# Moving loads of x, weights and first residuals in a cross-attention kernel

## The chip, the cores and the metric

The kernel runs on one core of a Trainium2 chip. The metric is device time in microseconds: the median of three runs. Beside it there is one profiled execution, whose time and span are given with it. The core's engines are PE (matrix products), DVE (reductions, transposes), ACT (ScalarE: copies out of PSUM, exponentials), POOL (elementwise work) and SP, which here only issues DMAs. ACT can issue DMAs too, in the order of its own instructions.

## What is computed

Two batches of 2048 tokens with 640 channels attend over 154 context rows, in 20 heads of 32 channels. The first 77 context rows and the last 77 have their own key and value weights and their own softmax; the two results are added, projected by Wo, and bias and residual are added.

```
q      = split_heads(x @ Wq.T)
k, v       = split_heads(text @ Wk.T),   split_heads(text @ Wv.T)     # context rows 0..76
k_ip, v_ip = split_heads(ip @ Wk_ip.T),  split_heads(ip @ Wv_ip.T)    # context rows 77..153
out = merge_heads(softmax(q k^T * s) v) + merge_heads(softmax(q k_ip^T * s) v_ip)
return out @ Wo.T + bo + x
```

## The kernel before

All matrices lie transposed in memory, channels first, in float32. Tokens are cut into four blocks of 1024 (`NBLK`), each of two halves of 512 (`TB`, `NH`). Channels are cut into five groups of 128 (`NC`), each of which is four heads (`G`).

The main loop has 20 iterations and one more to drain: iteration m handles block j = m // 5 and channel group c = m % 5. On PE it does the scores of 8 token tiles in three groups (3, 3 and 2 tiles, `scores(m, 0..2)`), and `attend(m - 1)`, the product of the iteration before's probabilities with V. Between those stands other PE work, which `plan(m)` lists in two parts, `after1` and `after2`. In iterations 0 to 4 these are a query projection for a later iteration, the V projections of group m, the K projections of group m + 1 and another query projection. Later they are query projections and output projections (`fill`). The order on every engine is the order of the program text; nothing reorders it.

ACT copies scores out of PSUM (`take`), computes the exponentials (`exponential`, part of `soften`), and copies queries, K, V and attention results out of PSUM. DVE does row maxima, sums, reciprocals, transposes of probabilities, and the last step of the output (`store`, line 319: PSUM result plus bias plus residual). POOL subtracts the maxima and multiplies by the reciprocals. A PSUM bank is used again once the engine that reads it is done; `turn_to` gives out the low or high four banks.

`soften(m, 0)` stands between the pieces of `after1`: the variable `ahead` says how many of them come first. Where `after1` has more than one entry, 2 < m < 18 and c > 0, the last entry comes behind `soften(m, 0)`. At c = 0 (iterations 5, 10, 15), where `after1` is two query projections, both come first.

Loads before the change:

- Weights of K and V: 20 tiles of 512 KB, through five slots that lie in the space of `aTs[1]`. `project_kv` issues the next load (`load_w`) right behind its matmuls.
- V, squared up by a DVE transpose (`square_v`), is spread over partitions by 16 small DMAs from SBUF to SBUF (`spread_v`, 20 KB each, called "pieces" below) for each channel group, and again for the second batch later.
- x of the next block: two loads of 1280 KB (`load_x(j + 1, h)`), written in iterations with c = 1, that is 1, 6 and 11.
- Wo: one load at the end of iteration 4. It goes into `wo_ct`, which held the context, so it waits for the last K and V projection.
- Residuals (`fetch`): 256 KB for each output tile; `flush` fetches up to `FETCH` = 3 ahead of the outputs stored so far, behind each store. There are 40 output tiles.

All of these are on SP's queue, in the order of the text; an issue that has to wait for a semaphore holds up every issue behind it. On ACT's queue there are only the first five loads of `wq`. The program gives all DMAs eight completion semaphores in turn, so each one also waits until the one eight places before it in program order has landed.

Of the kernel before, what the change touches and what calls it, by code (L numbers as in the profile page):

```python
# [19 lines left out]
def kernel(  # L20
# [25 lines left out]
    nc = tc.nc  # L46
    P = 128
    NC = C // P
    NCC = CC // P
    G = P // D  # L50
    TB = 512
    NH = 2
    BLK = NH * TB
    NT = BLK // P
    NBLK = B * S // BLK
# [6 lines left out]
    NM = NBLK * NC  # L62
# [4 lines left out]
    FETCH = 3  # L67
# [12 lines left out]
    def turn_to(half, n=G):  # L80


        turn[:] = half[:1] if n == 1 else (half[: min(n, G) - 1] + half[-1:]) * 2

    def bank():
        return turn.pop(0)
# [5 lines left out]
    xs = [const.tile([P, NC, BLK], F32, name=f"x_{n}") for n in range(2)]  # L92
# [14 lines left out]
    wo = wo_ct.rearrange("p (k o) -> p k o", k=NC)  # L107
# [6 lines left out]
    def block_of(m):  # L114

        j, c = divmod(m, NC)
        return j, c, j * BLK // S
# [7 lines left out]
    def load_w():  # L125
        n = len(loaded)
        if n < len(wlist):
            src, c = wlist[n]
            w = wslots[n % len(wslots)]
            nc.sync.dma_start(  # L130
                out=w, in_=src[:, ts(c, P)].rearrange("(k p) o -> p k o", p=P)
            )
            loaded.append(w)

    def project_kv(n, t):

        out = bank()[:, : B * L].rearrange("p (b l) -> p b l", b=B)
        for k in range(NCC):
            nc.tensor.matmul(  # L139
                out, loaded[n][:, k, :], cT[:, k, :, t, :], start=(k == 0), stop=(k == NCC - 1)  # L140
            )
        load_w()
        return out

    def project_k(c, t):
        nc.scalar.copy(kT[:, c, :, t, :], project_kv(4 * c + t, t))  # L146

    def project_v(c, t):
        nc.scalar.copy(vTs[c % 2][:, :, ds(t * L, L)], project_kv(4 * c + 2 + t, t))

    def square_v(c):
        nc.vector.transpose(
            vS[:, c].rearrange("p b l -> p (b l)"),
            vTs[c % 2].rearrange("p b l -> p (b l)"),
        )

    def spread_v(c, b):

        for g in range(G):
            for r in range(G):  # L160
                nc.sync.dma_start(
                    out=v4[r * D : (r + 1) * D, c, g].rearrange("p k d -> p (k d)"),
                    in_=vS[g * D : (g + 1) * D, c, b],
                )


    def load_x(j, h):
        nc.sync.dma_start(
            out=xs[j % 2][:, :, ts(h, TB)],
            in_=xT[:, ds(j * BLK + h * TB, TB)].rearrange("(c p) s -> p c s", p=P),  # L170
        )

    qTs = {}

# [22 lines left out]
    def keys_of(m, s):  # L197
        return pb_of(m, s)[:, :, :, : 2 * L]
# [4 lines left out]
    def scores(m, s, ps):  # L203

        _, c, b = block_of(m)
        first, n = GROUPS[s]
        for t in range(n):
            h, st = divmod(first + t, TB // P)
            for g in range(G):
                nc.tensor.matmul(  # L210
                    ps[g][:, ts(t, 2 * L)],
                    qTs[(m, h)][g * D : (g + 1) * D, ts(st, P)],
                    kT[g * D : (g + 1) * D, c, b].rearrange("p t l -> p (t l)"),
                    start=True,
                    stop=True,
                )

    def take(m, s, ps):

        n = GROUPS[s][1]  # L220
        for g in range(G):
            nc.scalar.copy(  # L222
                keys_of(m, s)[:, :, g], ps[g][:, : n * 2 * L].rearrange("p (n l) -> p n l", n=n)
            )

    def maxima(m, s):
        n = GROUPS[s][1] * G
        mx = small.tile([P, n, 2], F32, tag=f"mx{n}", name=f"mx_{m}_{s}")
        nc.vector.tensor_reduce(mx, rows_of(m, s), AX.X, ALU.max)  # L229
        nc.gpsimd.tensor_tensor(  # L230
            rows_of(m, s), rows_of(m, s), mx.unsqueeze(3).to_broadcast([P, n, 2, L]), ALU.subtract
        )
# [21 lines left out]
    def soften(m, s):  # L254
        exponential(m, s)
        sums(m, s)
        normalise(m, s)

    def transpose(m, s):
        first, n = GROUPS[s]  # L260
        nc.vector.transpose(  # L261
            tT[:, first : first + n].rearrange("p n g k s -> p (n g k s)"),
            pb_of(m, s).rearrange("p n g l -> p (n g l)"),
        )
# [59 lines left out]
    outs = [Out(v) for v in range(NV)]  # L324
# [23 lines left out]
    def flush():  # L348
        for o in finished[len(stored) :]:
            o.store()  # L350
            stored.append(o)
            for o in outs[len(stored) : len(stored) + FETCH]:
                o.fetch()
# [15 lines left out]
    for k in (0, half):  # L369
        nc.sync.dma_start(  # L370
            out=wo_ct[:, ds(k * B * LT, half * B * LT)].rearrange("p (k n) -> p k n", k=half),
            in_=ctxT[ds(k * P, half * P), :].rearrange("(k p) n -> p k n", p=P),
# [17 lines left out]
    for t in range(2):  # L390
        project_k(0, t)

    def plan(m):

        q = [lambda h=h: queries(m + LEAD[h], h) for h in range(NH)]
        out = lambda: fill(NC)
        if m < NC:
            v = [lambda t=t: project_v(m, t) for t in range(2)]
            k = [lambda t=t: project_k(m + 1, t) for t in range(2) if m + 1 < NC]
            return q[:1] + v, k + q[1:]  # L400
        if m == NM - 1:
            return [out], [out] + [lambda: fill(NC - 1)] * OPEN
        if m == NM - 2:
            return [out], [out, q[1]]
        if m % NC == 0:
            return q, [out] * 2
        return [out, q[0]], [out, q[1]]

    def is_late(m):


        return m == NC or (m > NC and m % NC == 1)

    for m in range(NM + 1):
        j, c, _ = block_of(m)
        new = m < NM
        old = m >= 1
        after1, after2 = plan(m) if new else ([], [])
        flush()
        if new:  # L420
            for g, half in ((0, LOW), (1, HIGH)):
                scores(m, g, half)
            for g, half in ((0, LOW), (1, HIGH)):
                take(m, g, half)
        turn_to(LOW, len(after1))


        ahead = len(after1)
        if ahead > 1 and 2 < m < NM - 2 and c > 0:
            ahead -= 1  # L430
        short = new and (len(after1) == 1 or m == 0)
        late = is_late(m)
        if old and not late:
            transpose(m - 1, 2)
        if new:
            maxima(m, 0)
        if late:
            transpose(m - 1, 1)
        if new and not short:
            maxima(m, 1)  # L440
        if late:
            transpose(m - 1, 2)
        if c == 1 and j + 1 < NBLK:
            for h in range(NH):
                load_x(j + 1, h)
        for work in after1[:ahead]:
            work()
        flush()
        if new:
            if short:  # L450
                maxima(m, 1)
            else:
                soften(m, 0)
        for work in after1[ahead:]:
            work()
        flush()
        if m < NC:
            square_v(m)
            spread_v(m, 0)
        if new:  # L460
            scores(m, 2, HIGH)
        if old:
            attend(m - 1, LOW)
        if new:
            take(m, 2, HIGH)
            maxima(m, 2)
            if short:
                soften(m, 0)
                if old:
                    take_attention(m - 1, LOW)  # L470
            soften(m, 1)
            if short:
                soften(m, 2)
        if old:
            if not short:
                take_attention(m - 1, LOW)
            attended[(m - 1) // NC] += 1
            if (m - 1) // NC == NBLK // B - 1:
                spread_v((m - 1) % NC, 1)
        turn_to(HIGH, len(after2))  # L480
        if new:
            transpose(m, 0)
        for work in after2[:-1]:
            work()
        flush()
        if new and not short:
            soften(m, 2)
        for work in after2[-1:]:
            work()
        if m >= NC and (c == 0 or m == NM - 2):  # L490
            flush()
        if new and not is_late(m + 1):
            transpose(m, 1)
        if m == NC - 1:
            nc.sync.dma_start(out=wo, in_=WoT.rearrange("(c p) o -> p c o", p=P))
    turn_to(LOW)
    while len(finished) < NV:
        fill(NC)
# [33 lines left out]
```

## Time and profile before

| | us |
|---|---|
| median of 3 runs (lowest, highest) | 537.57 (536.95, 538.74) |
| the profiled execution | 538.22 |
| its span | 536.4 |
| PE works on the first projections from | 10.97 |
| first scores of iteration 0 | 24.6 |
| first scores of iteration 5 | 140.6 |
| last output matmuls end near | 532.8 |

The page gives busy time, shares and counts for each engine; a table of stretches gives the same for parts of the span, with the clock that PE was granted (1.00 is full) and the share of the 16 DMA engines that was busy. A matmul in float32 appears as two matmuls and two weight loads. A row of the timeline is: start, length, engine, line, operation, what it writes and reads, count, and in brackets the idle time of the engine before it and what ended that. "issue" there means that the profile shows nothing that the engine waited for. SPq and ACTq are the DMA issues of those engines. Some matmul records can be missing, so counts can be a few short.

DMA issues of the page that the change touches, with KB each and median us from issue to landing:

| load | issued by | count | KB | us |
|---|---|---|---|---|
| residuals | SP | 40 | 256 | 3.3 |
| x of the next block | SP | 6 | 1280 | 8.7 |
| V pieces | SP | 160 | 20 | 1.8 |
| weights of K, K_ip, V, V_ip | SP | 5 each | 512 | 7.0, 4.4, 5.5, 4.2 |
| Wo | SP | 1 | 1600 | 7.0 |

### The profile page before, as it was taken

The numbers are of one execution on the slowest core, as the hardware profiler recorded it, in microseconds if no ns is written. First come the engines' busy times: TensorE is split into PE (matmuls) and PEld (weight loads), VectorE is DVE, ScalarE is ACT, GpSimd is POOL, SyncE is SP. The second block draws the span as 40 slices with busy tenths as digits, with TensorE's granted clock in tenths as the row PEclk, the third lists the DMA queues.
The fourth block names the chain that finished last, engine by engine and source line by source line (L and its number), as shares of the span: only waits on it lengthen the run. The fifth ranks groups of instructions, "written<-read, shape, count | busy, mean of one in ns | idle before, by whom it ended". The sixth has DMA issues, their size and how long they took to land.

```text
span 536.4 us, 12754 instructions
## 1 busy us (share of the span) xinstructions
PE 522.8 (97%) x5614; PEld 289.0 (54%) x5614; DVE 378.1 (70%) x286; ACT 245.1 (46%) x441; POOL 351.0 (65%) x130
## 2 busy tenths in 40 slices
PE   8999799999999999999999999999999999999997
PEld 4676668677554545545454554544455454554442
DVE  0059765877878879787768978787678878888121
ACT  1255445456654444644454464445356464562000
POOL 0057947796967868668677866869576876978000
PEclk9999799999999999999999999999999999999999
DMA  8974733320136420221206311111112111131151
GB/s 258 308 208 138 243 94 88 97 59 9 32 138 221 150 89 25 82 65 48 57 16 221 144 41 40 42 39 42 38 41 75 45 42 40 40 101 40 61 187 67
DMA packets 50488, 50.60 MB, mean 94 GB/s; under 512 B 5248, under 2 KB 34432, under 8 KB 50432
## 3 DMA queue, kind: packets, MB, share of 16 engines
q1 hardware_dynamic: 49712, 49.45, 30.3%
q8 instruction: 44, 0.72, 0.6%
q10 hardware_dynamic: 720, 0.33, 0.2%
q14 instruction: 12, 0.10, 0.1%
HBM read 36.00 MB, written 10.49 MB: 87 GB/s over the span
## 4 chain that ended last, share of the span: by engine, by line
PE 87%; DVE 4%; issue 2%; DMA 2%; POOL 2%; ACT 1%; SPq 0%; ACTq 0%; DVEq 0%; POOLq 0%
PE bank L181 30%; PE bank L308 30%; PE bank L273 11%; PE bank L210 8%; PE bank L139 8%; DVE den L243 2%; POOL pb L250 2%; DVE mx L229 1%; DMA x<-in_x_dram 1%; ACT pb L236 1%; DVE ot L319 1%; DMA wq<-in_L_xattn_Wq_dram 1%; DMA res<-in_x_dram 1%; POOL pb L230 0%; DVE tT L261 0%
## 5 line engine op out<-in xcount | busy, mean ns | idle before, releaser
L230 POOL TENSOR_TENSOR pb<-pb,mx 128x1848 f32<-128x1848 f32 (+1 forms) x60 | 175.8, 2942 | 105.9 <-DVE mx L229 105.9
L250 POOL TENSOR_TENSOR pb<-pb,rden 128x1848 f32<-128x1848 f32 (+1 forms) x60 | 176.0, 2942 | 36.9 <-DVE rden L245 27.7
L181 PE MATMUL bank<-x,wq 128*128 128x512 f32 x400 | 180.0, 599 | 0.9 <-DMA x<-in_x_dram 0.9
L308 PE MATMUL bank<-aT,wo_ct 128*128 128x512 f32 x400 | 179.1, 599 | 0.9 <-ACT aT L285 0.9
L243 DVE TENSOR_REDUCE den<-pb 128x24 f32<-128x1848 f32 (+1 forms) x60 | 111.3, 1856 | 62.3 <-ACT pb L236 62.2
L229 DVE TENSOR_REDUCE mx<-pb 128x24 f32<-128x1848 f32 (+1 forms) x60 | 109.6, 1848 | 43.3 <-ACT pb L222 42.3
L236 ACT ACTIVATE pb<-pb 128x1848 f32<-128x1848 f32 (+1 forms) x60 | 95.1, 1587 | 87.4 <-POOL pb L230 87.4
L181 PEld LDWEIGHTS bank<-x,wq 128*128 128x128 f32 x400 | 75.4, 191 | 92.8 <-issue 87.4
L308 PEld LDWEIGHTS bank<-aT,wo_ct 128*128 128x128 f32 x400 | 73.7, 190 | 91.8 <-issue 83.8
L261 DVE STREAM_TRANSPOSE tT<-pb 128x1920 f32<-128x1920 f32 (+1 forms) x60 | 115.9, 1931 | 5.3 <-POOL pb L250 5.2
L222 ACT COPY pb<-bank 128x462 f32<-128x462 f32 (+1 forms) x240 | 101.1, 533 | 22.5 <-PE bank L210 21.2
L273 PE MATMUL bank<-tT,v 32*32 32x256 f32 x3200 | 70.5, 386 | 4.1 <-issue 3.6
L189 ACT COPY qT<-bank 128x512 f32<-128x512 f32 x40 | 23.4, 585 | 99.5 <-PE bank L181 99.5
L210 PEld LDWEIGHTS bank<-kT,qT 32*128 32x128 f32 x1280 | 44.7, 184 | 30.2 <-issue 19.6
L273 PEld LDWEIGHTS bank<-tT,v 32*32 32x32 f32 x3200 | 46.9, 103 | 21.9 <-issue 8.7
L210 PE MATMUL bank<-kT,qT 32*128 32x154 f32 x1280 | 54.8, 303 | 2.5 <-DVE ot L319 1.9
L319 DVE SCALAR_TENSOR_TENSOR ot<-bank,bo_sb,res 128x512 f32<-128x512 f32 x40 | 29.5, 739 | 37.6 <-PE bank L308 31.9
L139 PEld LDWEIGHTS bank<-wo_ct,aT 128*128 128x128 f32 x320 | 45.5, 197 | 5.2 <-issue 3.3
L139 PE MATMUL bank<-wo_ct,aT 128*128 128x154 f32 x320 | 46.9, 305 | 0.5 <-ACT pb L222 0.5
L285 ACT COPY aT<-bank 128x256 f32<-128x256 f32 x80 | 24.4, 391 | 17.2 <-PE bank L273 17.2
L245 DVE RECIPROCAL rden<-den 128x24 f32<-128x24 f32 (+1 forms) x60 | 17.2, 286 | 2.1
L146 ACT COPY kT<-bank 128x154 f32<-128x154 f32 x10 | 2.8, 286 | 15.1 <-PE bank L139 15.1
(12 smaller groups left out, 14.0 us busy)
## 6 DMA issues: line engine op xcount, KB each, us to landing
res<-in_x_dram SPq DMA_DIRECT2D x40, 256.0 KB, 3.3
out_dram<-ot SPq DMA_DIRECT2D x40, 256.0 KB, 2.4
x<-in_x_dram SPq DMA_DIRECT2D x6, 1280.0 KB, 8.7
v<-vS SPq DMA_DIRECT2D x160, 20.0 KB, 1.8
x<-in_x_dram SPq DMA_DIRECT2D x10, 256.0 KB, 5.0
aT<-in_L_xattn_Wk_dram SPq DMA_DIRECT2D x5, 512.0 KB, 7.0
aT<-in_L_xattn_Wk_ip_dram SPq DMA_DIRECT2D x5, 512.0 KB, 4.4
aT<-in_L_xattn_Wv_dram SPq DMA_DIRECT2D x5, 512.0 KB, 5.5
```

The costliest lines, as they stand in the source:

```text
L139: nc.tensor.matmul(out, loaded[n][:, k, :], cT[:, k, :, t, :], start=(k == 0), stop=(k == NCC - 1))
L181: nc.tensor.matmul(pq, wq[:, k, ts(c, P)], xs[j % 2][:, k, ts(h, TB)], start=(k == 0), stop=(k == NC - 1),)
L210: nc.tensor.matmul(ps[g][:, ts(t, 2 * L)], qTs[(m, h)][g * D : (g + 1) * D, ts(st, P)], kT[g * D : (g + 1) * D, c, b].rearrange("p t l -> ...
L222: nc.scalar.copy(keys_of(m, s)[:, :, g], ps[g][:, : n * 2 * L].rearrange("p (n l) -> p n l", n=n))
L229: nc.vector.tensor_reduce(mx, rows_of(m, s), AX.X, ALU.max)
L230: nc.gpsimd.tensor_tensor(rows_of(m, s), rows_of(m, s), mx.unsqueeze(3).to_broadcast([P, n, 2, L]), ALU.subtract)
L236: nc.scalar.activation(e, e, AF.Exp, scale=SCALE)
L243: nc.vector.tensor_reduce(den, rows_of(m, s), AX.X, ALU.add)
L250: nc.gpsimd.tensor_tensor(rows_of(m, s), rows_of(m, s), rdens[s].unsqueeze(3).to_broadcast([P, n, 2, L]), ALU.mult)
L261: nc.vector.transpose(tT[:, first : first + n].rearrange("p n g k s -> p (n g k s)"), pb_of(m, s).rearrange("p n g l -> p (n g l)"),)
L273: nc.tensor.matmul(pa[r][g * D : (g + 1) * D, : NT * D], v4[rows, c, g, k, :], tT[rows, :, g, k, :], start=(k == 0), stop=(k == NK - 1),)
L308: nc.tensor.matmul(self.po, wo[:, self.k, ts(self.o, P)], aTs[self.j % 2][:, self.k, ts(self.h, TB)], start=(self.k == 0), stop=(self.k == ...
```

## The change

- `load_w()` leaves `project_kv`. It is called in `project_k`, behind its copy, and twice in each `spread_v(c, 0)`, behind pieces 4 and 8. So the weights that V projections used to issue now stand among the pieces.
- In `spread_v(4, 0)` the load of Wo and the fetches of residuals 0 to 2 stand behind piece 4, ahead of the 12 other pieces. They leave the end of iteration 4 and the first stores.
- x of the next block is cut into ten slices of 256 KB (one channel group of one half each), issued by ACT, up to three in an iteration, behind the takes of groups 0 and 1. The list is filled in iterations 1, 5 and 10. So slices are written in iterations 1 to 4 (3, 3, 3, 1), 5 to 8 and 10 to 13.
- The condition c > 0 for `ahead` is dropped: in iterations 5, 10 and 15 the second query projection is written behind `soften(m, 0)`.

```diff
@@ project_kv, project_k
-        load_w()
         return out

     def project_k(c, t):
         nc.scalar.copy(kT[:, c, :, t, :], project_kv(4 * c + t, t))
+        load_w()
@@ spread_v
                     in_=vS[g * D : (g + 1) * D, c, b],
                 )
+            if b == 0 and g < 2:
+                load_w()
+            if (b, c, g) == (0, NC - 1, 0):
+                nc.sync.dma_start(out=wo, in_=WoT.rearrange("(c p) o -> p c o", p=P))
+                for o in outs[:FETCH]:
+                    o.fetch()
@@ load_x
-    def load_x(j, h):
-        nc.sync.dma_start(
-            out=xs[j % 2][:, :, ts(h, TB)],
-            in_=xT[:, ds(j * BLK + h * TB, TB)].rearrange("(c p) s -> p c s", p=P),
-        )
+    slices = []
+
+    def load_x():
+        if slices:
+            j, h, k = slices.pop(0)
+            nc.scalar.dma_start(
+                out=xs[j % 2][:, k, ts(h, TB)], in_=xT[ts(k, P), ds(j * BLK + h * TB, TB)]
+            )
@@ main loop
         flush()
+        if m == 1 or (m >= NC and c == 0 and j + 1 < NBLK):
+            slices.extend((j + 1, h, k) for h in range(NH) for k in range(NC))
...
                 take(m, g, half)
+            for _ in range(3):
+                load_x()
         turn_to(LOW, len(after1))

         ahead = len(after1)
-        if ahead > 1 and 2 < m < NM - 2 and c > 0:
+        if ahead > 1 and 2 < m < NM - 2:
             ahead -= 1
...
-        if c == 1 and j + 1 < NBLK:
-            for h in range(NH):
-                load_x(j + 1, h)
...
-        if m == NC - 1:
-            nc.sync.dma_start(out=wo, in_=WoT.rearrange("(c p) o -> p c o", p=P))
```

## The prediction

> **What bounds the kernel.** I read the page's busy shares first, then busy time stretch by stretch, one iteration m of the main loop at a time, then PE's own order of time where a stretch is long.
>
> ```profile
> PE 522.8 (97%) x5614; PEld 289.0 (54%) x5614; DVE 378.1 (70%) x286; ACT 245.1 (46%) x441; POOL 351.0 (65%) x130
> PEclk9999799999999999999999999999999999999999
> ```
>
> PE is the bound, so only PE's gaps and its slow stretches can be won. The fifth digit of the granted clock (53.6 to 67.0 us) is the only one below 9. Stretches, each from the first scores of an iteration to the next ones (columns: PE, PEld, DVE, ACT, POOL busy, clock, DMA share, GB/s):
>
> ```profile
> 45.08:74.48 29.40, 26.70 (x309) 19.26 (x308) 20.90 (x16) 13.06 (x25) 21.31 (x8) 0.88 0.60 179
> 74.48:97.73 23.25, 23.25 (x310) 16.69 (x309) 16.32 (x12) 12.87 (x25) 16.05 (x6) 1.00 0.36 97
> ...
> 164.46:189.74 25.28, 23.99 (x269) 12.30 (x268) 21.86 (x18) 11.50 (x20) 20.09 (x8) 1.00 0.55 187
> 189.74:213.14 23.40, 23.40 (x269) 11.95 (x268) 18.85 (x15) 11.98 (x21) 17.52 (x7) 1.00 0.19 60
> ```
>
> Iterations 1 and 2 do the same work on PE, yet 1 takes 6.15 us more. Iterations 6 and 7 do the same, yet 6 takes 1.88 us more. These two places hold nearly all there is to win. The first one, in PE's order of time:
>
> ```profile
> 56.30 3.22 PE L273 MATMUL bank<-tT,v 32*32 32x256 f32 x141
> 62.23 1.12 PE L273 MATMUL bank<-tT,v 32*32 32x256 f32 x19 [2.71 <-issue]
> 63.28 6.98 PE L139 MATMUL bank<-wo_ct,aT 128*128 128x154 f32 x32
> ...
> 80.66 4.38 PE L139 MATMUL bank<-wo_ct,aT 128*128 128x154 f32 x32
> ```
>
> PE stops in the middle of attend(0), 141 of its 160 matmuls done, for 2.71 us and waits for nothing that the profile names; the 32 projections behind it then take 6.98 us instead of 4.38. The stretches around it:
>
> ```profile
> 53.00:59.50 6.50, 6.50 (x178) 5.12 (x176) 3.31 (x3) 2.92 (x6) 5.66 (x2) 1.00 1.06 383
> 59.50:62.30 2.80, 0.10 (x12) 0.07 (x16) 2.77 (x4) 2.56 (x5) 1.67 (x2) 0.88 1.16 289
> 62.30:68.50 6.20, 6.20 (x39) 5.39 (x40) 5.06 (x4) 1.32 (x5) 6.20 (x3) 0.50 0.17 40
> ```
>
> The DMA engines are full (share over 1, 383 GB/s) until the gap ends, and after it PE has half its clock for 6.2 us. The kind of packet that is missing is code: the page's row below is some 255 PE instructions a packet (2 x 5614 over 44), the DMA view shows no packet of this queue between 50.6 and 59.4 us and one from 59.4 to 61, and attend issues 320 instructions in 3.3 us, more than a packet's worth. I read the gap as PE out of code, because the next packet stood behind the traffic that SP issued:
>
> ```profile
> q8 instruction: 44, 0.72, 0.6%
> ```
> ```profile
> 48.05 2.37 SPq L168 DMA_DIRECT2D x<-in_x_dram  x2
> 53.56 0.37 SPq L130 DMA_DIRECT2D aT<-in_L_xattn_Wv_ip_dram  x1
> 55.67 0.37 SPq L130 DMA_DIRECT2D aT<-in_L_xattn_Wk_dram  x1
> ...
> 146.31 0.52 SPq L303 DMA_DIRECT2D res<-in_x_dram  x1
> 162.72 0.36 SPq L322 DMA_DIRECT2D out_dram<-ot  x1
> 163.12 1.39 SPq L303 DMA_DIRECT2D res<-in_x_dram  x3
> ```
>
> That is 2 x 1280 KB of x and 2 x 512 KB of weights at 48 to 56 us, on top of two weights at 47. The last three lines are the second place: SP fetches residual 0, then waits 16 us with the store of output 0, so residual 1 starts only at 163.12; the bias-and-residual step waits for it, and PE's scores wait for the bank which that step frees:
>
> ```profile
> 166.27 0.75 DVE L319 SCALAR_TENSOR_TENSOR ot<-bank,bo_sb,res 128x512 f32<-128x512 f32 x1 [1.20 <-DMA res<-in_x_dram]
> ```
> ```profile
> 167.08 1.05 PE L210 MATMUL bank<-kT,qT 32*128 32x154 f32 x18 [1.29 <-DVE ot L319]
> ```
>
> **The change part by part.** On PE, DVE and POOL the order of instructions stays as it was; only ACT's order and the two DMA queues change.
>
> *Traffic of iteration 1.* SP's first piece of V(0) leaves at 36.12 and 16 take 10.62, 0.66 each. Two weights now stand among them: one after piece 4 (38.8 us; lands in 4.2 to 7.0, needed by the projections at 53.4), the next after piece 8. Pieces and weights end near 48, two more weights leave by 49.5, and three 256 KB slices of x follow ScalarE's last take (46.16 + 3.68 = 49.84). From 48 on that is 1.8 MB instead of 4.6; at 383 GB/s it is over by 54.5. The next pieces wait for V(1)'s squares until 61.75, and the later weights stand behind those. PE stops 282 instructions into attend; one packet (255) back, some 0.2 us into attend (56.5), it can have asked for the next, which now meets idle engines. A small wait can stay: iteration 16 has one of 0.66 at full clock under little traffic (135 GB/s), there 274 instructions into attend and over at 417.07, 3.4 us after the like point (413.6). Here 56.5 + 3.4 = 59.9, 0.4 after the code ends at 59.52. Other iterations show less, down to none. Gain 6.15 less 0 to 0.66; I take 0.4: **5.75**. Of the 6.15, 2.71 is the gap and 3.4 the half clock behind it, which a gap of 0.66 did not bring.
>
> The Trainium skill, Runtime: NRT & Kernel Launch, "Instruction fetch mechanics", says code is refilled in blocks of 256 instructions while the current one runs, mostly hidden; the 2.71 us gap is the exception here. By that rule taken alone the gap is not code and the sum below would lose its first term, 535.3.
>
> *First residuals and Wo.* Residuals 0 to 2 are now issued some 25 us before use, so the 1.20 wait at 166.27 ends, and with it the 1.29 on PE. What is left of the 1.88 is scores waiting for the same bank while DVE does sums; iteration 11, where residuals are early, still has 0.48 of that (2.33 for its 48 scores against 1.85 in iteration 10). Gain 1.4 to 1.88; with the next part, **1.8**.
>
> *Exponential ahead of the second query copy in iterations 5, 10, 15.* Now it starts when POOL is done (149.06 + 0.04 in iteration 5) instead of 152.22, some 3 us earlier; sums and the outputs' step follow on DVE, so the second output's bank is free when scores come. The copy moved behind it ends before 152.4, as before: POOL's release plus 1.75 is 150.9, PE's result 151.74. Worth at most the 0.48 of iteration 11 and 0.11 of iteration 16: **0.5**, bounds 0 and 0.6.
>
> *x on ScalarE's queue.* 30 slices; five wq issues on that queue took 2.34, so 0.47 each, 1.4 us for three. They stand ahead of the query copy; in iteration 1 ScalarE idles 1.61 us there waiting for PE, so **0**; at SP's price for the same slices (10 in 6.57, so 2.0 for three) 0.4 is over that slack and may reach PE once. Bounds 0 and 0.5. Each slice also waits until the DMA eight before it has landed (eight completion semaphores in turn). In iteration 2 these are pieces 9 to 11 of V(1): from 61.75, behind 8 pieces and two weights (0.53 each), and one of them behind a weight issued at 64.4 (4.2 to land) they leave by 70.4 and land by 72.2; ScalarE's takes end there at 74.48 + 4.76 - 6.15 = 73.1, so no wait.
>
> The skill's DMA: Bandwidth & Descriptors, "Issuing engines are not separate DMA queues", speaks against this part: another issuing engine saves only issue time. By it the move alone is worth SP's 2.37 us of issuing, which is off the path, so nothing; 383 GB/s in the gap agrees that engines, not a queue, were full.
>
> *Wo inside the last spreading.* Clock of before: piece 1 at 134.82, piece 4 ends 137.5, Wo is issued and lands 7.0 later, 144.5. Pieces 5 to 8 go meanwhile; piece 9 must wait for Wo, 10 to 12 for the residuals (256 KB at 383 GB/s: 0.7 each), 13 to 16 follow; the last is issued at 149.2 and lands 1.8 later, 151.0. attend(4) needs it at 152.4: **0**, slack 1.4. At 292 GB/s and 2.7 us landings, as in the loaded window, it would be 154.7: a loss of 2.3. The slices of iteration 5 wait for pieces 9 to 11, so ScalarE stands until 148.2 and the query copy of 147.44 slips to 148.2; the exponential waits for POOL until 149.1 anyway. 0.
>
> **Sum.** 5.75 + 1.8 + 0.5 = 8.05. The profiled execution of 538.22 (span 536.4 and 1.8 around it) becomes 530.2, its span 528.4. It is 0.65 over the median 537.57, so the median is forecast at **529.5**.
>
> **Rivals.** (A) *The gap is a fixed code wait, or only halves.* For it: iteration 16's gap without load. Against: that one is 0.66, and 2.9 us of the packet's wait coincide with full engines. Then 537.57 - 2.3 = 535.3. (B) *PE's lead is given back by softmax.* The gap let the softmax of iteration 1 catch up. Its last exponential can start when POOL's subtraction ends (64.74 + 2.25 = 67.0 instead of 70.48), so only 3.5 of the 6.15 come along; if PE paid the other 2.7: 532.2. Against: sums, POOL's products and the last transpose then end at 69.7, 72.5 and 74.0, and attend(1) comes at 85.7 - 6.15 = 79.5; DVE is busy 16.3 of 23.25 in iteration 2 and gains on PE. (C) *Wo holds up V(4): slower.* Place: attend(4) in iteration 5. Each us that Wo lands later than 1.4 us past plan is a us on PE, and the gap of iteration 1 shows 3.4 more for the clock. Slower than before begins when stall and clock eat 8.05, at a stall of 4.65: Wo landing 13.1 us after issue instead of 7.0. At a stall of 8.5 (8.5 + 3.4 - 8.05): 541.4. Against: 2.4 MB at the slowest rate seen is 8.2 us.
>
> **How the numbers follow.** Forecast 0.78, B 0.08, A 0.09, C 0.05. The likeliest case's bounds: at best 6.15 + 1.88 + 0.6, less the runs' own 0.6, is 528.3; at worst 5.49 + 1.4 + 0, less 0.5 for ScalarE and half of Wo's 2.3, is 532.3. For what else can happen the range goes a little lower, to 527.7, and up over B, to 533.2. Under 0.3% (1.6 us) no change can be told. Faster is the forecast, A and B (0.95), less A's outcomes with hardly a gain (0.03): 0.92; same is those and C's mildest (0.01): 0.04; slower the rest of C: 0.04.
>
> **What would show it.** Right: attend in iteration 1 in one piece of about 3.4 us, the projections behind it at 4.4, all clock digits 9, stretch 1 near 23.5; no wait of line 319's step for a residual; scores of iteration 6 in 1.8. Wrong: a gap over 1 us in attend(0); attend(4) waiting for v; ScalarE idle behind slices while PE waits for its copies; a clock digit below 9 past the start.

## The result and the profile after

The changed kernel takes 532.80 us (median of 6 runs, 531.13 to 534.36), the kernel before beside it 537.37 (536.73 to 539.90). The ratio is 0.9908, 95% interval 0.9878 to 0.9937. The profiled execution took 532.77 us, its span 531.0, which is 5.4 less than before, where the prediction's sum had 8.05.

The page of the changed kernel, busy time and granted clock:

```profile
PE 520.4 (98%) x5614; PEld 285.6 (54%) x5614; DVE 378.7 (71%) x286; ACT 245.8 (46%) x441; POOL 351.0 (66%) x130
PEclk9999999999999999999999999999999999999999
```

PE is still the bound, and the slow digit of before is gone. The stretches of the changed kernel, same columns as before (PE, PEld, DVE, ACT, POOL busy, clock, DMA share, GB/s), for iterations 1, 2, 5, 6, 7 and 18:

```profile
44.43:67.80 23.37, 23.37 (x310) 16.74 (x309) 18.35 (x14) 12.97 (x25) 18.66 (x7) 1.00 0.47 134
67.80:91.04 23.24, 23.24 (x309) 16.69 (x308) 18.76 (x14) 13.04 (x25) 18.53 (x7) 1.00 0.53 143
134.43:159.72 25.29, 24.98 (x265) 12.11 (x264) 19.67 (x15) 12.84 (x23) 21.49 (x8) 1.00 0.44 153
159.72:183.24 23.52, 23.52 (x266) 12.07 (x265) 20.36 (x16) 11.40 (x20) 17.40 (x7) 1.00 0.28 91
183.24:206.64 23.40, 23.40 (x266) 11.95 (x265) 19.70 (x15) 11.98 (x21) 18.01 (x7) 1.00 0.29 94
443.29:464.13 20.84, 19.46 (x255) 9.94 (x254) 16.35 (x14) 11.54 (x20) 15.53 (x6) 1.00 0.08 27
```

And the last of these as it was in the kernel before:

```profile
449.88:469.17 19.29, 19.18 (x256) 10.05 (x256) 15.25 (x13) 11.55 (x20) 13.97 (x6) 1.00 0.09 29
```

Iterations 1 and 6 are as short as their neighbours now. Iterations 5 and 18 are longer than before. Lengths of iterations (from the first scores of one to those of the next, read from PE's timeline; iterations not shown are within 0.15 of before):

| iteration | before | after | difference |
|---|---|---|---|
| start, up to the first scores | 24.59 | 23.95 | -0.64 |
| 1 | 29.40 | 23.37 | -6.03 |
| 3 | 23.82 | 24.35 | +0.53 |
| 5 | 23.88 | 25.30 | +1.42 |
| 6 | 25.21 | 23.51 | -1.70 |
| 11 | 23.87 | 23.51 | -0.36 |
| 16 | 24.46 | 24.76 | +0.30 |
| 18 | 19.29 | 20.85 | +1.56 |
| 19 and the outputs behind it | 63.00 | 62.61 | -0.39 |

The start is not the change's doing: among runs whose program is the same up to there it lies between 23.57 and 24.59. The places in PE's order of time, changed kernel:

```profile
55.65 3.51 PE L283 MATMUL bank<-tT,v 32*32 32x256 f32 x160
59.09 4.49 PE L139 MATMUL bank<-wo_ct,aT 128*128 128x154 f32 x32
...
102.27 3.59 PE L283 MATMUL bank<-tT,v 32*32 32x256 f32 x160
106.80 4.38 PE L139 MATMUL bank<-wo_ct,aT 128*128 128x154 f32 x32 [0.94 <-ACT aT L295]
...
146.21 4.81 PE L283 MATMUL bank<-tT,v 32*32 32x256 f32 x160
...
159.72 1.96 PE L220 MATMUL bank<-kT,qT 32*128 32x154 f32 x48
...
450.47 2.99 PE L283 MATMUL bank<-tT,v 32*32 32x256 f32 x136
454.73 0.69 PE L283 MATMUL bank<-tT,v 32*32 32x256 f32 x24 [1.27 <-issue]
```

First pair: attend(0) runs in one piece, and the projections behind it take 4.49 us instead of 6.98. The 146.21 row: attend(4) takes 4.81 instead of 3.39, so it waits inside. The 159.72 row: the scores of iteration 6 take 1.96 in one piece. The last pair: a new hole of 1.27 us in attend(17), again with nothing that the profile names.

Why attend(4) waits is in the chain of waits of the changed kernel (start, length, what):

```profile
133.73 8.59 DMA res<-in_x_dram
...
144.79 2.70 DMA v<-vS
147.49 3.52 PE bank L283 x125
```

The third residual lands 8.59 us after its issue, at 142.32. One piece waits for that, the last four stand behind it, and the last one lands at 147.49, 1.28 us after attend(4) began.

### The profile page after: what moved, and what is told of

Same layout as the page of the kernel before. It is cut to its first block, busy times and chain, and to the rows that moved or that the text cites. A ratio compares the mean times of both kernels' runs of the same rounds, so it can differ in the third digit from the quotient of the medians.

```text
span 531.0 us, 12772 instructions
## 1 busy us (share of the span) xinstructions
PE 520.4 (98%) x5614; PEld 285.6 (54%) x5614; DVE 378.7 (71%) x286; ACT 245.8 (46%) x441; POOL 351.0 (66%) x130
## 4 chain that ended last, share of the span: by engine, by line
PE 89%; DMA 4%; POOL 2%; DVE 2%; SPq 1%; ACT 1%; issue 1%; ACTq 0%
PE bank L318 33%; PE bank L191 29%; PE bank L283 12%; PE bank L220 8%; PE bank L139 7%; DMA res<-in_x_dram 2%; POOL pb L240 1%; SPq L161 1%; DMA x<-in_x_dram 1%; ACT pb L246 1%; DMA wq<-in_L_xattn_Wq_dram 1%; DMA v<-vS 1%; DVE ot L329 0%; POOL pb L260 0%; DVE den L253 0%
## 5 line engine op out<-in xcount | busy, mean ns | idle before, releaser
L283 PE MATMUL bank<-tT,v 32*32 32x256 f32 x3200 | 71.7, 385 | 2.8 <-issue 2.4
L139 PEld LDWEIGHTS bank<-wo_ct,aT 128*128 128x128 f32 x320 | 43.1, 188 | 5.8 <-issue 4.5
L139 PE MATMUL bank<-wo_ct,aT 128*128 128x154 f32 x320 | 44.3, 294 | 1.4 <-ACT aT L295 0.9
L149 ACT COPY vT<-bank 128x154 f32<-128x154 f32 x10 | 2.9, 287 | 13.2 <-PE bank L139 13.2
```

The source lines that it names most:

```text
L139: nc.tensor.matmul(out, loaded[n][:, k, :], cT[:, k, :, t, :], start=(k == 0), stop=(k == NCC - 1))
L283: nc.tensor.matmul(pa[r][g * D : (g + 1) * D, : NT * D], v4[rows, c, g, k, :], tT[rows, :, g, k, :], start=(k == 0), stop=(k == NK - 1),)
```

## The experiments

Each kernel is the one before or the changed one with one edit, or with the two or three that are named. Where a kernel ran only once, its time stands beside a run of the kernel before on the same chip, and the verdict rests on the lengths of iterations, which agree within some 0.02 us wherever nothing is late. Holes vary more: the changed kernel and its version with Wo first (section 4) have the same program before iteration 4, and there iteration 1 took 23.37 and 23.91, iteration 3 24.35 and 23.80.

### 1. Is the gap of iteration 1 traffic, or PE's place in its code?

Two kernels ran for this. The first moves the bulk x of iteration 1 into iteration 2:

```diff
-        if c == 1 and j + 1 < NBLK:
+        if (m == 2 or (c == 1 and j > 0)) and j + 1 < NBLK:
```

> The kernel before, with one edit: the two 1280 KB loads of x that it writes in iteration 1 are written in iteration 2. PE's instructions are the same. Theory (code packet late because SP's traffic fills the DMA engines): the gap in attend(0) shrinks to under 0.7 us, the clock stays full, and iteration 1 falls from 29.4 us to 23.3 to 24.1; the span falls by some 5.5 to 6. Rival (a code wait fixed by the place of the packet's edge, whatever the traffic): iteration 1 stays at 29.4.

The second leaves all loads as they are and puts 27 tiny matmuls in place of two of the seven that warm PE up, 100 instructions more, so every later instruction stands elsewhere in PE's code:

```diff
-    for _ in range(7):
+    for _ in range(27):
+        nc.tensor.matmul(LOW[0][:D, :D], warm[:D, :D], warm[:D, :D], start=True, stop=True)
+    for _ in range(5):
```

> The kernel before, with its loads as they were, but 27 tiny matmuls ahead of the warming ones and 5 warming ones in place of 7: 100 more PE instructions at the start, which moves the edges of all code packets by 100 instructions. Theory (PE runs out of code inside attend(0) because the packet's edge lies there while traffic is heavy): with the edge elsewhere the same traffic costs nothing, iteration 1 falls to 23.3 to 24, and waits of 0.2 to 1.5 us each without a named cause turn up behind the attends whose edge now falls like that of attend(0) (executed in iterations 8 to 10), while those of iterations 14 to 16 go. Rival (the gap is something else that traffic holds up, such as data of V or weights): iteration 1 stays above 28.

With x moved, iteration 1 took 24.47 (hole 0.71 us, clock full), a little above the 23.3 to 24.1 expected. The total was 534.72 beside 537.0, so the span gained less than the 5.5 to 6 expected, because iteration 6 grew to 27.32: its wait for the bank, 1.29 before, was 1.70, and PE lost clock behind it. With the code shifted, iteration 1 took 23.24 under unchanged traffic. But the total was 536.91: the padding put the first scores 1.14 later, iterations 2, 8 and 9 grew by 0.55 to 1.01, and the largest hole, more than was expected anywhere, stood in iteration 11. PE's timeline of the kernel with the shifted code:

```profile
57.44 3.38 PE L273 MATMUL bank<-tT,v 32*32 32x256 f32 x160
60.75 4.48 PE L139 MATMUL bank<-wo_ct,aT 128*128 128x154 f32 x32
...
291.93 2.79 PE L273 MATMUL bank<-tT,v 32*32 32x256 f32 x132
296.90 1.15 PE L273 MATMUL bank<-tT,v 32*32 32x256 f32 x28 [2.19 <-issue]
```

Iteration 11 took 27.44 instead of 23.87. Its hole stands beside the next bulk load of x (issued at 283.72) and a store with a residual (291.5 to 292.3). So a hole of this size needs both conditions: traffic, and an attend at a bad place in the code. With x out of the way a bad place still gave 0.71 here. The packets of the instruction queue say the same. The DMA view of the kernel before for 59 to 60 us, inside its hole (queue: packets, MB, share of the engines):

```profile
q8 instruction: 1, 0.02, 7.2%
```

The changed kernel, 56 to 57 us, while attend(0) runs:

```profile
q8 instruction: 1, 0.02, 5.8%
```

The kernel with the shifted code, 55 to 56 us, before attend(0) begins at 57.44:

```profile
q8 instruction: 1, 0.02, 6.7%
```

In the kernel before, attend(0) begins at 56.30, so the packet comes 2.7 to 3.7 us into it; in the changed one 0.4 to 1.4 us (from 55.65). With shifted code it is moved, at 389 GB/s of other traffic, before attend(0) begins.

The packets' own times say more. In the kernel before, the packet is transferred from 59.49 to 60.64, and PE goes on at 62.23; in attend(17) of the changed kernel from 452.01 to 453.46, and PE goes on at 454.73; with shifted code from 294.27 to 295.28, and PE goes on at 296.90. The traces of the 13 kernels have 42 holes of 0.15 us or more in or right behind an attend that the profile puts down to no transfer. Each of them ends 1.2 to 1.6 us after the end of a packet of this queue.

### 2. Which part of the change ends it?

Two parts, each put alone into the kernel before. First the slices of x on ACT's queue (`load_x` rewritten as in the change):

```diff
-        if c == 1 and j + 1 < NBLK:
-            for h in range(NH):
-                load_x(j + 1, h)
+        if m == 1 or (m >= NC and c == 0 and j + 1 < NBLK):
+            slices.extend((j + 1, h, k) for h in range(NH) for k in range(NC))
...
+            for _ in range(3):
+                load_x()
```

> The kernel before with the x of later blocks in slices on ScalarE's queue and nothing else of the change. Theory (attend(0) of iteration 1 waits for a code packet that stands behind whatever traffic is outstanding when TensorE asks for it): the slices leave less in flight than two bulk loads, but the weights are still loaded in the same microseconds, so iteration 1 lies between the two kernels: 24.0 to 27.5 us (29.40 before, 23.37 after); iteration 6 stays near 25.2, since Wo and the first residuals are where they were; iterations 14 to 18 each move by up to 1 us either way, because four waits fewer on TensorE shift the packets' edges. Rival (the shape and queue of the x load are the whole of it, weights play no part): iteration 1 is 23.4 as after.

Then the weights among V's pieces:

```diff
-        load_w()
         return out
...
+        load_w()
...
+            if b == 0 and g < 2:
+                load_w()
```

> The kernel before with the K and V weights moved behind V's pieces and nothing else of the change (x stays in two bulk loads on SyncE's queue in iteration 1). Theory of outstanding traffic: 1.57 MB of x plus the pieces is enough to hold the packet for part of the time: iteration 1 is 24 to 28 us; with the weights' two loads out of iteration 0 the start keeps 24.6. Rival (x's bulk load alone makes the gap): iteration 1 stays at 29.4. Second rival (the weights alone make it): 23.4. Iterations 6 and 11 stay at 25.2 and 23.9 on every theory.

Iteration 1 took 24.41 with the slices alone (total 531.73 beside 538.56) and 27.76 with the weights alone (535.12). PE's timeline, slices alone:

```profile
59.48 0.68 PE L277 MATMUL bank<-tT,v 32*32 32x256 f32 x19 [0.66 <-issue]
60.09 4.49 PE L139 MATMUL bank<-wo_ct,aT 128*128 128x154 f32 x32
```

Weights alone:

```profile
61.47 0.68 PE L275 MATMUL bank<-tT,v 32*32 32x256 f32 x19 [2.35 <-issue]
62.08 6.14 PE L139 MATMUL bank<-wo_ct,aT 128*128 128x154 f32 x32
```

The second row of each pair shows why the slices bring most: behind the hole of 0.66 the projections take 4.49, as without a hole, and behind the one of 2.35 they take 6.14, at a lower clock. The hole of 0.66 is dearer than it looks all the same: with it iteration 1 is 1.17 longer than the 23.24 that it takes with no hole. Of the 6.03, the slices alone bring 4.99, the weights alone 1.64. With the slices alone, iteration 5 took 24.67, because Wo, still at its old place, held up the first output by 0.74 us; iteration 6 then took 24.28, not the 25.2 expected, though its residual was still fetched behind the first output's store. I take this as a sign that time which PE loses in iteration 5 shortens iteration 6. The total of the slices alone, 531.73 in one run, is no higher than the 532.80 of the whole change.

### 3. Does the issuing queue matter?

The changed kernel with its slices on SP's queue:

```diff
-            nc.scalar.dma_start(
+            nc.sync.dma_start(
```

> The changed kernel with the same slices at the same places, but issued on SyncE's queue. Theory (what counts is bytes ahead of the packet, not which engine issued them): iteration 1 is 23.3 to 24.0 as in the changed kernel (23.37), total 531 to 534. Rival (moving x off SyncE's queue is what frees the packet): iteration 1 is above 25 us. In iteration 5 ScalarE no longer issues the slices, so its 5.68 us wait for a transfer goes, but V's pieces land late as before: 24 to 26 us (25.30).

Iteration 1 took 23.36 (23.37 with ACT's queue): the queue is not what frees the packet. Iteration 5, however, took 23.94, better than "V's pieces land late as before". SP's and PE's timeline of this version:

```profile
145.61 1.53 SPq L179 DMA_DIRECT2D x<-in_x_dram  x3
```

```profile
146.12 3.44 PE L283 MATMUL bank<-tT,v 32*32 32x256 f32 x160
```

The slices leave behind the last piece, and attend(4) waits for nothing. In the changed kernel ACT sends them at 143.22, while SP still has pieces to issue (ACT's timeline, then SP's):

```profile
143.22 1.64 ACTq L179 DMA_DIRECT2D x<-in_x_dram  x3
144.90 0.58 ACT L199 COPY qT<-bank 128x512 f32<-128x512 f32 x1 [5.68 <-DMA v<-vS]
```

```profile
132.12 0.53 SPq L168 DMA_DIRECT2D wo_ct<-in_L_xattn_Wo_dram  x1
132.69 1.57 SPq L313 DMA_DIRECT2D res<-in_x_dram  x3
134.31 11.08 SPq L161 DMA_DIRECT2D v<-vS  x12
```

768 KB overtake the last pieces; at the 383 GB/s seen under full load they occupy the engines for an estimated 2.05 us. Without them the pieces, issued no earlier, come in time. The total, 532.05 beside 538.56, is hardly below the changed kernel's: the holes of section 5 remain.

### 4. Wo and the first residuals

The changed kernel with Wo ahead of the 16 pieces and the residuals behind them:

```diff
+        if (b, c) == (0, NC - 1):
+            nc.sync.dma_start(out=wo, in_=WoT.rearrange("(c p) o -> p c o", p=P))
...
-            if (b, c, g) == (0, NC - 1, 0):
-                nc.sync.dma_start(out=wo, in_=WoT.rearrange("(c p) o -> p c o", p=P))
-                for o in outs[:FETCH]:
-                    o.fetch()
+        if (b, c) == (0, NC - 1):
+            for o in outs[:FETCH]:
+                o.fetch()
```

> The changed kernel, with the load of Wo ahead of the 16 pieces of V(4) instead of behind the fourth, and the three residuals behind the last piece. Theory (pieces 9 to 12 wait for Wo and the residuals, which land some 2 us later than forecast, and attend(4) waits for them): iteration 5 falls from 25.30 us to 23.4 to 23.9 and ScalarE's 5.7 us wait for v goes; iteration 6 stays at 23.5. Rival (attend(4) is late by the order of ScalarE's work in iteration 5): iteration 5 stays above 25.

Iteration 5 took 23.88 and the total was 531.42. SP's timeline and PE's of this version:

```profile
125.54 0.37 SPq L160 DMA_DIRECT2D wo_ct<-in_L_xattn_Wo_dram  x1
```

```profile
145.77 3.39 PE L284 MATMUL bank<-tT,v 32*32 32x256 f32 x160
```

Wo leaves 6.6 us earlier, while SP has nothing else to issue, and the pieces follow it without a wait. So the 1.42 of iteration 5 took two things together, Wo and the residuals among the pieces and the slices that overtook the last ones: with either removed it is gone.

Iteration 6 has two candidates, the early residuals and the exponential moved ahead. The exponential alone, in the kernel before:

```diff
-        if ahead > 1 and 2 < m < NM - 2 and c > 0:
+        if ahead > 1 and 2 < m < NM - 2:
```

> The kernel before with the exponential of group 0 ahead of the last projection or fill in the iterations with c = 0 too, and nothing else. TensorE's instruction count and the packets' edges are those of before. Theory: iteration 11 goes from 23.87 to 23.4-23.6, iteration 16 from 24.46 by 0 to 0.3 less, iteration 6 from 25.21 by 0 to 0.5 less, everything else within 0.1 (iteration 1 29.4): total 536.0 to 537.0 beside 537.4. Rival (the exponential ahead does nothing; what shortened iterations 6 and 11 was the earlier Wo and the x in slices): 6, 11 and 16 within 0.1 of before.

And the changed kernel without it (the same lines the other way round):

> The changed kernel without its third part: in the iterations with c = 0 the exponential of group 0 is behind the second query copy again. TensorE's instruction count is that of the changed kernel. Theory A (the exponential is the lever; in the kernel before it alone brought iteration 6 from 25.21 to 23.82, with the residual still late): iteration 6 is 24.5 to 25.3, iterations 11 and 16 lose 0.3 to 0.5 each. Theory B, as the prediction has it (the first residuals, now issued 25 us ahead, end the wait): iteration 6 is 23.5 to 24.0, and only iterations 11 and 16 lose 0.3 to 0.5 each.

The exponential alone: iteration 6 at 23.82, 11 at 23.50, 16 at 23.94, more gained than expected in 6 and 16 (total 535.20 beside 538.56; a start of 23.73 instead of 24.59 is part of that). DVE's and PE's timeline of that version:

```profile
164.07 0.75 DVE L319 SCALAR_TENSOR_TENSOR ot<-bank,bo_sb,res 128x512 f32<-128x512 f32 x1 [2.23 <-DMA res<-in_x_dram]
```

```profile
163.65 2.28 PE L210 MATMUL bank<-kT,qT 32*128 32x154 f32 x48
```

DVE still waits for the residual, longer than before (2.23 against 1.20). But output 0, behind whose store SP fetches that residual, is stored at 160.24 instead of 162.72, so this step ends 1.17 us after the scores began (163.65 to 164.82) instead of 2.56 (164.46 to 167.02), and the scores run through in 2.28. Without the exponential but with the early residuals, iteration 6 took 23.50, 11 took 23.86 and 16 took 24.21; total 533.13 beside 537.23. That is theory B's number for iteration 6, but this run does not show that the residuals alone suffice: its iteration 5 took 25.79, PE stood there waiting for v, and by section 2 such a stand shortens iteration 6. What it does show is that in iteration 6 the step of line 329 no longer waits for a residual but for PE:

```profile
160.13 0.75 DVE L329 SCALAR_TENSOR_TENSOR ot<-bank,bo_sb,res 128x512 f32<-128x512 f32 x1 [1.37 <-PE bank L318]
```

The nearest case without such a stand is iteration 11 of the kernel before, with early residuals and the old order: 23.87. By it the residuals alone would bring iteration 6 to an estimated 23.9. Iteration 16 became shorter than in the changed kernel (24.76), not 0.3 to 0.5 longer: its hole was 0.18 instead of 0.73.

### 5. The holes of iterations 3, 16 and 18

The traces have 56 waits for semaphores on PE before and 46 after, beside the same 5614 matmuls and 5614 weight loads: ten waits have dropped out with the loads that moved (with the slices alone four, with the weights alone five). From iteration 2 on each attend therefore stands 1 to 10 instructions earlier in PE's code. Counting from the start of the program's stream modulo 256, attend(17) begins at 192 before and at 182 after (the rows of the traces, which lack a few entries of the stream, give places 4 or 5 lower). A record of attend is two instructions, a matmul and its weight load, so the place where PE stops can be worked out from the rows:

| run, iteration | attend begins at | records until the hole | PE stops at (mod 256) |
|---|---|---|---|
| before, 1 | 170 | 141 | 452, that is 196 |
| after, 18 | 182 | 136 | 454, that is 198 |
| slices alone, 1 | 170 | 141 | 452, that is 196 |
| shifted code (+100), 11 | 189 | 132 | 453, that is 197 |
| 6 tiny matmuls (below), 13 | 142 | 155 | 452, that is 196 |

PE stops at the same point of 256 every time, to within two instructions; so it does at all 42 holes of section 1. I take that point for the end of a code packet. Where two such points fall into one attend (3.4 us for 320 instructions) the second packet has little time to come. Attend(2) of the changed kernel begins at 132 and ends at 452, so its hole of 0.94 stands just behind it. The kernel before has that hole too, 0.19 in its profiled run and 0.41 in the run with the exponential alone, with the same code and loads up to there, so the longer iteration 3 is at least in part chance. The profile names ACT's copies of attention results there, but in the program those projections wait only for ACT's takes of scores.

First test, 192 instructions more, again in place of warming matmuls:

```diff
-    for _ in range(7):
+    for _ in range(52):
+        nc.tensor.matmul(LOW[0][:D, :D], warm[:D, :D], warm[:D, :D], start=True, stop=True)
+    for _ in range(3):
```

> The changed kernel with 192 more PE instructions at the start (52 tiny matmuls, 3 warming ones in place of 7), nothing else. Theory (the changed kernel has 10 PE instructions fewer by iteration 18, semaphore waits that fell away; that moves the edges of code packets, and so brings the waits of 0.94 us in iteration 3 and 1.27 in iteration 18 beside those of 0.2 to 0.7 in 14 to 16): iterations 3, 14 to 16 and 18 fall to 23.8, 23.4, 23.4, 23.6 to 24 and 19.3, some 3.5 to 4 us in all, and attends of iterations 4 to 6 may pay 0 to 0.7 each. Rival (those waits have to do with the data or with ScalarE, which the profile names in iteration 3): they stay.

Iterations 3, 14, 15, 16 and 18 took 23.24, 23.40, 23.39, 23.50 and 19.28: the holes went. But iteration 2, of which nothing was expected, took 24.88 (a hole of 1.05, at position 197 again, though only one such point lies in that attend), iteration 5 took 24.51, and the padding put the first scores at 27.28. Total 532.18: nothing won.

Then a padding that should cost next to nothing: tiny matmuls where PE waits 0.38 us for kT before the first scores, and Wo ahead as in section 4. With 6 of them:

```diff
     for t in range(2):
         project_k(0, t)
+    for _ in range(6):
+        nc.tensor.matmul(LOW[0][:D, :D], warm[:D, :D], warm[:D, :D], start=True, stop=True)
```

> The changed kernel with Wo issued ahead of the last spreading's 16 pieces (residuals behind them), and 6 tiny matmuls (24 instructions of TensorE) put where it waits for kT before the first scores, so that all later code-packet edges lie 24 instructions elsewhere; they should cost 0 to 0.6 us there. The attends of blocks 15 to 18 leave the bad positions (170-186 of 256 become 194-210), those of 12, 13 and 14 stand at 142, 160 and 178. Theory: iterations 16 and 18 fall to 23.4-23.9 and 19.3, iteration 13 or 14 or 15 lose 0.5 to 1.0 each, at most 1.8 together, iteration 5 is 23.9: total 528.3 to 530.3, that is 1 to 3 us below the version with Wo first alone (531.42). Rival (the gaps of iterations 16 and 18 come from the traffic of stores and residuals alone, wherever the edges lie): 531 to 532.

With 12:

> The same with 12 tiny matmuls (48 instructions): the attends of blocks 15 to 18 stand at 218, 234, 230 and 226, those of 11, 12 and 13 at 148, 166 and 184, that of block 2 at 180 instead of 132. Theory: the code waits move to iterations 12 to 14 at 0.1 to 1.0 us each, iteration 3 loses its 0.5, the padding costs 0.3 to 1.2 at the start: total 528.3 to 530.5. Rival as for the other: 531 to 532.5.

The version with 6 took 528.72 us (median of 4 runs, 528.00 to 529.48; ratio to before 0.9850, interval 0.9814 to 0.9886), that with 12 took 528.88 (528.76 to 529.21; 0.9850, 0.9821 to 0.9878). The version with 6 is 2.7 us below the one run with Wo first alone, and the difference lies in the holes: with 6, iterations 1, 14, 15, 16 and 18 took 23.24, 23.50, 23.69, 23.51 and 19.28 (23.91, 24.18, 24.30, 24.48 and 20.57 there), and the padding moved the first scores by 0.1 to 0.2, less than runs differ there. New ones stand about where the theory puts them, iteration 13 at 24.55 with 6 tiny matmuls, 12 and 13 at 24.38 and 23.89 with 12. Two things went otherwise with 12: iteration 3 kept 23.93, and iteration 11 took 23.84. PE's timeline with 6:

```profile
336.24 0.62 PE L284 MATMUL bank<-tT,v 32*32 32x256 f32 x5 [0.58 <-issue]
...
446.85 3.39 PE L284 MATMUL bank<-tT,v 32*32 32x256 f32 x160
```

attend(17) runs in one piece; the hole in attend(12) is at position 196. Both versions beat the two kernels compared here.

## Why the prediction was right, and where its sum was off

The forecast, 529.5, was 3.3 us too low: of the 8.05 us forecast, 4.57 came. 532.80 lies within the range, 0.4 below its upper end, and that is partly luck. It is above the 532.3 that the likeliest case allowed; the range went up to 533.2 to cover rival B, which did not happen, and what used most of that room was a loss that the prediction had not seen. The kernel is faster by the means that were named, with costs beside them that were not.

*Traffic of iteration 1 (5.75).* Right: 6.03. That PE was out of code was argued from one packet and one count; the shifted code shows it, since the hole went with no load moved, and so do the packets that precede the end of every hole. (The 383 GB/s stood ahead of the gap; in it there were 289.) The 0.4 that was kept for a residual hole hardly came in this run, but iteration 1 of the version with Wo first, at 23.91, has it. Where a hole of 0.66 does come, it costs 1.17, so the bound of 0.66 was too low. The Trainium skill, Runtime: NRT & Kernel Launch, "Instruction fetch mechanics", has code refilled in blocks of 256 instructions. The stops at 196 to 198, all at one place of 256, agree. The page calls the cost of a refill mostly hidden. That fits most of the 44 or 45 packets of each run, but in every version some hole shows; the longest of each lasts from 0.42 us (12 tiny matmuls) to 2.71 (before). "Mostly" leaves room for such holes, so the rule taken alone did not strike out the first term, contrary to what the prediction says.

*First residuals, Wo and the exponential (1.8, and 0.5 for 11 and 16).* Iterations 6 and 11 gave 1.70 and 0.36. The prediction gave the larger share to the residuals. The exponential alone, with the residual still late, brought iteration 6 to 23.82; what the residuals bring alone is not shown. Iteration 16 gained nothing on the whole. Where it has no hole it takes 23.87 in the old order (shifted code) and 23.50 in the new one (192 instructions more), so the exponential is worth 0.37 there, and in the changed kernel a longer code wait took more than that back.

*x on ScalarE's queue (0, to 0.5) and Wo inside the last spreading (0, slack 1.4).* These are the first mis-sized terms: together they cost 1.42, within the bounds given (2.3 for Wo). Shifted to the changed kernel's clock (iteration 5 starts 6.15 us earlier), the plan had the residuals landed by 140.5 and the last piece by 144.9. They landed at 142.3 and 147.5: the residuals' own delay used up the slack, and the last piece took 2.70 to land instead of 1.8. The plan timed the pieces behind Wo and the residuals, but let the slices cost only ACT's time; that they leave before the last pieces and take the engines from them was missing. On SP's queue, behind the pieces, they cost nothing here. So rival C's mechanism is real, with a stall of 1.28 us where 4.65 would have made the kernel slower. The Trainium skill, DMA: Bandwidth & Descriptors, "Issuing engines are not separate DMA queues", was weighed against this part and agrees with the runs: with the slices on SP's queue iteration 1 is the same to 0.01 us. What the second issuing engine changed here is the order, and here it let 768 KB overtake what SP still had to send.

*"On PE, DVE and POOL the order of instructions stays as it was."* This is the step that failed. The order did stay; the number of PE's instructions did not, and with it the place of each attend in the code. It is a term that the sum did not have: 1.56 in iteration 18. That loss is no chance: the four kernels with the changed code at this place took 20.57 to 20.87 there, the five in which attend(17) stands 5 to 11 instructions later took 19.28 or 19.29, and padding brought 19.28 back. Code waits also cost 0.53 in iteration 3 and took back the gain of iteration 16, but these two differ between runs of the same code by about as much. With the 1.42 of iteration 5, and 0.54 missing in iterations 6, 11 and 16, that makes 4.05. Iteration 1 gave 0.28 more than forecast, and the start and the end gave 1.0 back. What is left is about the 2.6 us by which the profiled execution lies above its forecast.

*Rivals.* A (a fixed code wait) fell: the hole went from 2.71 to 0.66 and to nothing with the load. B (PE's lead given back) fell: iteration 2 took 23.25 as before.

## What to carry to other kernels

A hole on PE that the profile puts down to nothing can be code that comes late; count PE's instructions up to the hole in two places, and if the counts agree modulo 256, move the code by a few instructions or the traffic by a few microseconds. Any edit that adds or drops instructions or waits on PE, even ones that take no time, moves these points for the whole rest of the program, so compare versions iteration by iteration. A load given to a second issuing engine gets no engines of its own; ask which transfers it will now overtake. And compare a hole's cost in whole iterations: it can be more than the idle time that the profile shows.

## What the hardware showed

Whether a pause of PE costs the clock too went with its length here. Behind pauses of 0.66, 1.27 and 1.33 us the clock stayed full; behind 1.70, 2.19, 2.35, 2.45 and 2.71 us it fell to half. Stretches behind the 1.27 of the changed kernel and the 2.19 of the kernel with 100 instructions more (clock in the third column from the right):

```profile
454.73:458.00 3.27, 3.27 (x30) 1.46 (x31) 1.30 (x2) 2.56 (x4) 3.27 (x3) 1.00 0.02 8
```

```profile
296.90:300.00 3.10, 3.10 (x31) 1.26 (x32) 2.18 (x3) 1.73 (x5) 3.10 (x3) 0.50 0.04 9
```

Ten waits that take no time of their own cost 1.3 to 1.6 us by their absence (iteration 18), and six tiny matmuls won more back (528.72 as a median against one run of 531.42). From the end of a code packet's transfer to PE's next matmul it took 1.2 to 1.6 us in all 42 holes. Why the hole in iteration 2 of the version with 192 instructions more came with only one packet's end in its attend stays open, as does exactly when PE asks for a packet.
